# The end of the first slot in a four-stage kernel: batch 2's products, the weights and the transposed output in another order

## The chip, the cores and the metric

One core of a Trainium2 chip runs the whole program. The metric is the time of one execution on the device in microseconds, given as the median of several. The engines that matter here are TensorE (PE in the profile, with its weight loads as PEld), VectorE (DVE), ScalarE (ACT), GpSimd (POOL), and SyncE's queue (SP), from which most DMAs are issued. Each engine works through its own queue in order, and waits at an instruction until the semaphores that it needs are set.

## The reference

The input is four batches of 512 rows by 256 columns in fp32. Each is normalised and passed through four sublayers, each added to its own input:

```python
x = x + attn_a(layernorm(x))     # windows
x = x + ffn(layernorm(x))
x = x + attn_b(layernorm(x))     # causal attention
x = x + ffn(layernorm(x))
```

`attn_a` cuts a batch into tokens of 16 channels, makes q, k, v of each, and attends within windows of eight tokens in two branches (eight along one axis for the first eight channels, eight along the other for the rest). A 3x3 depthwise convolution of v is added, and the result is projected by a 16x16 matrix, normalised over its 16 channels and added to the normalised input. `ffn` has 2048 hidden units; gate, up and down weights are 4-bit codes with a scale for each block of 32:

```python
gate = einsum('th,nh->tn', xt, Wg);  up = einsum('th,nh->tn', xt, Wu)
out = einsum('tn,hn->th', gelu(gate) * up, Wd)
```

`attn_b` has 16 heads of 16 channels, with rotary positions and a causal mask.

## The kernel before, in words

All four batches stay in SBUF as `X[b]` ([128, 4, 256]). The weights are unpacked once, on VectorE, into `Wf`: twelve words (`WORDS`, L720: g0, u0, ... d2, d3), each of six VectorE steps and two DMA loads from SP's queue (`dequant`, L722). The buffers of the later words come from pools with two turns, so that a word's loads wait until the word two before it has been used up.

The work is laid out in slots. In a slot TensorE runs one batch's FFN pass (`ffn`, L824) while the other engines work on another batch's windows:

- before the slots: batch 0's windows, alone
- first slot: FFN of batch 0 (pass f0), windows of batch 1, the start of batch 2's windows, and the second half of the weights (`first_slot`, L1393)
- two further slots: FFN of batch 1 with the windows of batch 2 (pass f1), FFN of batch 2 with those of batch 3
- then the remaining FFN passes with the causal attention beside them

A pass has two halves of eight hidden tiles. For tile n, TensorE makes `pg_n` (gate) and `pu_n` (up), each of two 128x512 matmuls (two records each in the trace); ScalarE applies gelu to `pg_n` into `gs_n`; VectorE multiplies `it_n = pu_n * gs_n` (L866 in the first slot, L868 later). At the end of a half, four `po` groups of eight 128x256 matmuls take all eight `it`, and VectorE adds each `po` to X (L897). `pg`, `pu` and `po` share three PSUM banks in turn (pool `ps3`, L69): a tile may be written only when the tile three before it has been read. So gate tile n+2 waits for `it_n`.

The windows of a batch are: `window_front` (statistics of the 16-token rows, normalisation, transposes `yTp`, q, k, v and convolution into T); `window_parts` (L433), that is products of q and k (`tq`), folded into scores (`sc`), their maximum (`mx`), exponentials (`ek`), weighting of v (`tv`), and sums into `att`; `window_back` (L640), that is for each half a transpose `aTp` (L655), a copy `aT` by ScalarE (L657), a projection (L661), and statistics; then `turn` (a root by Newton steps on 128x64, scalings, and `z`), `move` (`zp`: 64 narrow matmuls that bring z into X's layout, L700) and `add` (X <- X + zp, L711). `norm_rows` (L759) makes the next pass's input of X: four statistics (L771, L772), the root (L777 and, on GpSimd, L778), four `xn` (L789), their transposes `xTp` (L809), and ScalarE's copies `xT` (L812, L813).

Sums over eight products are made in one of two ways: by VectorE, folding halves (`fold`, `values_here`), or on TensorE, piling eight products and the convolution up in a PSUM bank by matmuls with the identity (`pile`, `values_piled`, L588). In the first slot, the values of branch 1, half 0, are piled in the bank `va1`.

What sets the order: in the first slot the queues of TensorE and VectorE are written out by hand, with a planner. `Pace` (L104) keeps two running times, `pe` and `dve`. VectorE work is booked with `spend` (L126), which lets the pass take further steps (`steps`, each `each` us of TensorE) as long as `pe` is behind `dve`, and issues an `it` when its due time has come. `matmuls` books other TensorE work. `fill` (L1409) puts weight steps (`pieces`) among the products up to a cap on the number made, `want` makes a word at the latest when the pass needs it, and `step` advances the front of batch 2. After the first slot, `weave` (L1220) writes out TensorE's queue alone, and the other engines' queues follow a scheduler; `queue_behind` (L1232) ties an instruction behind another in the issue order, with no wait of its own. `beside_window` (L1491) runs `window_middle` (L609), whose first products of batch b are tied behind `state[b - 1, "moved"]` (the last z) for half 0 and behind `state["f..."]` (the last `xn` of the coming pass) for half 1.

Of the kernel before, what the change touches and what calls it, by code (L numbers as in the profile page):

```python
# [14 lines left out]
ALU = mybir.AluOpType  # L15
# [20 lines left out]
def hybrid_kernel(  # L36
# [25 lines left out]
    nc = tc.nc  # L62
# [80 lines left out]
    def paced(us):  # L143

        if pace:
            pace[0].spend(us)
            if pace[0].fill is not None:
                pace[0].fill()
# [138 lines left out]
    def window_front(a1, a2, c, b, y, state):  # L287
# [12 lines left out]
        if b in (1, 2):  # L300

            junk = a1.tile([P, P], F32, tag="junk", name=f"junka{b}")
            for s in range(8):
                if b == 2 and s == 4:
                    yield 2.5
                nc.scalar.activation(junk, y[:, s, :], AF.Identity, accum_out=mv[:, s, 0:1])
            yield 3.5
            ps = over_halves(0, mv[:, :, 0])
            nc.scalar.activation(mean, ps, AF.Copy, scale=-1.0 / P)
            yield 1.0  # L310
            for s in range(8):
                if b == 2 and s == 4:
                    yield 2.5
                nc.scalar.activation(
                    junk, y[:, s, :], AF.Square, bias=mean[:, s : s + 1], accum_out=mv[:, s, 1:2]
                )
            yield 3.5
            nc.scalar.activation(off, over_halves(1, mv[:, :, 1]), AF.Copy, scale=1.0 / P)
            inv_root(rs, off)
            nc.gpsimd.tensor_tensor(mean, mean, rs, ALU.mult)  # L320
            yield 3.0
        else:
            for s in range(8):
                st = a2.tile([P, 6], F32, tag="st", name=f"sta{b}_{s}")
                nc.vector.bn_stats(st, y[:, s, :])
                nc.vector.bn_aggr(mv[:, s, :], st)
            yield 3.5
            if b == 0:
                busy(8)
            mm = over_halves(0, mv.rearrange("p s t -> p (s t)")).rearrange("p (s t) -> p s t", t=2)  # L330
            nc.vector.tensor_tensor(off, mv[:, :, 0], mm[:, :, 0], ALU.subtract)
            nc.vector.tensor_tensor(off, off, off, ALU.mult)
            nc.vector.scalar_tensor_tensor(off, off, EPS, mm[:, :, 1], ALU.add, ALU.add)
            nc.gpsimd.tensor_tensor(rs, off, mhalf, ALU.pow)

            yield 4.0
            yield 4.0
            behind = last_on(mybir.EngineType.DVE).name
            ins = nc.vector.scalar_tensor_tensor(mean, mm[:, :, 0], -1.0, rs, ALU.mult, ALU.mult)
            if b > 1:  # L340
                queue_behind(ins, behind)
# [42 lines left out]
        for hf in range(2):  # L384
# [13 lines left out]
            for s in range(max(lo - 1, 0), min(hi + 1, 7) + 1):  # L398
                t0, t1 = max(0, lo - s + 1), min(3, hi + 2 - s)
                at = 384 + 16 * (s - 1 - lo)  # L400
# [32 lines left out]
    def window_parts(a1, a2, c, b, state):  # L433
# [22 lines left out]
        def pile(dst, parts):  # L456
            for n, part in enumerate(parts):
                nc.tensor.matmul(dst, ident, part, start=n == 0, stop=n == len(parts) - 1)  # L458
# [127 lines left out]
            paced(0.35)  # L586

        def values_piled(br, hf, at=None):  # L588
            part = tmp["v", br, hf]
            if at is not None:  # L590
                got["va", br] = at
            dst = bank("va", br)[:, 256 * hf : 256 * hf + 256]
            own = T[:, hf, 7 - br]
            pile(dst, [part(k, k + 1)[:, :, 0] for k in range(8)] + [own])

        def take_piled(br, hfs):
            rows = slice(4 * hfs[0], 4 * hfs[-1] + 4)
# [11 lines left out]
    def window_middle(a1, a2, c, b, state):  # L609

        w = window_parts(a1, a2, c, b, state)

        def late(br):

            behind = last_on(mybir.EngineType.Activation).name
            queue_behind(w["power"](br), behind)

        for br in range(2):
            for hf in range(2):
                ins = w["products"](br, hf)  # L620
                if br == 0:

                    queue_behind(ins, state[b - 1, "moved"] if hf == 0 else state[f"f{b - 1}"])
                w["scores_here"](br, hf)
                yield 4.6
            w["peak"](br)
            yield 1.4

        late(0)
        late(1)  # L630
        for br in range(2):
            w["total_here"](br)
            w["shares"](br)
            yield 2.3
            for hf in range(2):
                w["weighted"](br, hf)
                w["values_here"](br, hf)
                yield 5.1
# [593 lines left out]
    def queue_behind(ins, name):  # L1232

        tc.add_manual_dep(
            ins.ins, name,
            mybir.DependencyInfo(mybir.DependencyClass.NoSync, mybir.DependencyReason.DATA),
            reason="issue order",
        )
# [12 lines left out]
    def drain(work):  # L1251
        for _ in work:
            pass
# [37 lines left out]
    with ExitStack() as left:  # L1291
# [101 lines left out]
        def first_slot():  # L1393


            run = Pace()
            run.each = 0.9
            run.main = ffn(f1, i1, 0, got[0], "f0", False, False, later=run)
            xa = window_load(a2, 2)
            other = window_front(a1, a2, wconst, 2, xa, state)  # L1400
            w = window_parts(a1, a2, wconst, 1, state)
            first_made = made[0]

            def pieces(n, us=0.6):
                for _ in range(n):
                    if next(words, None) is not None:
                        run.spend(us)

            def fill():  # L1409

                while made[0] < min(0.8 * run.dve + first_made - 4.0, 66):
                    pieces(1)

            def want(name):
                while made[0] < 6 * WORDS.index(name) + 6:
                    next(words)
                    run.dve += 0.6

            run.want = want

            def step(costs=[0.0, 0.0, 0.2, 0.0, 0.0, 0.2, 0.0, 0.0, 0.9, 3.7, 2.5]):
                next(other, None)
                if costs:
                    run.matmuls(costs.pop(0))

            pace.append(run)
            run.fill = fill
            for br in range(2):
                for hf in range(2):
                    w["products"](br, hf)  # L1430
                    w["scores_here"](br, hf)
                    step()
                w["peak"](br)
                step()
            behind = last_on(mybir.EngineType.Activation).name
            queue_behind(w["power"](0), behind)
            queue_behind(w["power"](1), last_on(mybir.EngineType.Activation).name)
            pieces(4)
            for br in range(2):
                w["total_here"](br)  # L1440
                w["shares"](br)
                if br == 0:
                    step()
                for hf in range(2):
                    w["weighted"](br, hf)
                    if br == 0:
                        step()
                    if (br, hf) == (1, 0):
                        w["values_piled"](br, hf, one("va1"))
                        run.matmuls(4.2)  # L1450
                        w["take_piled"](br, (hf,))
                        continue
                    if (br, hf) == (1, 1):
                        project, turn, move, add = window_back(a1, a2, wconst, 1, state)
                        first, second = project(0), project(1)
                        next(first)
                        run.matmuls(0.5)
                    w["values_here"](br, hf)
                    if br == 0:
                        step()  # L1460
            next(first)
            run.matmuls(0.9)
            next(second)
            run.matmuls(0.5)
            run.fill = None
            next(first, None)
            next(second)
            run.matmuls(0.9)
            run.limit = 96
            pieces(72 - made[0])  # L1470
            next(second, None)
            next(second, None)
            drain(turn())
            run.spend(6.2)
            move()
            run.matmuls(3.8)
            pieces(72)
            run.limit = 96
            run.spend(max(0.0, run.pe - run.dve))
            add()  # L1480
            run.spend(1.2)
            for _ in norm_rows(f1, 1, "f1", got, aside=lambda: run.spend(2.0)):
                run.spend(0.45)
            run.room(0)
            pace.clear()
            for _ in run.main:
                pass
            run.room(0)
            del state["due"]
# [146 lines left out]
```

## Time and profile before

| | |
|---|---|
| median of 3 runs | 1032.29 us (1028.6 to 1038.07) |
| profiled execution | 1030.32 us, of which its span 1028.4 us |
| busy: PE, DVE, ACT, POOL | 98%, 65%, 34%, 13% of the span |
| granted TensorE clock, mean | 0.991 |
| first slot's pass on TensorE | from 82.3 us to 193.1 us |
| HBM traffic | 12.32 MB read, 2.10 MB written |

A row of a timeline gives start and length in us, engine, line, operation, output and inputs with their shapes, the number of records, and in brackets the idle time before it and what ended that. TensorE's rows overlap a little where matmuls are pipelined. A row of the waits gives who waited for whom, the total in us, the number of times and the longest. In a table by stretches the clock is the share of full speed that TensorE was granted.

### The profile page before, as it was taken

Reading aid. Unit: us, or ns where it says so; the run is one execution under the profiler, and the core shown is the slowest. Engines: PE = TensorE matmul, PEld = TensorE weight load, DVE = VectorE, ACT = ScalarE, POOL = GpSimd, SP = SyncE. Lnnn points to the kernel's source line nnn. Section 1 sums busy time; section 2 is a strip of 40 time slices with the busy share of each in tenths; the row PEclk is TensorE's granted clock in tenths of the full one; section 3 lists DMA queues with packets and bytes.
Section 4 is the critical chain, followed back from the end, with each engine's and each line's share of the span. In section 5 each row is a group of like instructions: output and inputs, shape, how many; then the busy total and the mean of one; then the engine's idle time right before and its main releaser. Section 6 shows DMA issues by size and latency. Waiting matters only on the chain.

```text
span 1028.4 us, 14319 instructions
## 1 busy us (share of the span) xinstructions
PE 1005.5 (98%) x5574; PEld 596.2 (58%) x5574; DVE 670.7 (65%) x1589; ACT 350.9 (34%) x603; POOL 132.4 (13%) x259
## 2 busy tenths in 40 slices
PE   7989999899999999999999999999999999999998
PEld 7864657565756475564474554664644746446556
DVE  6978999958866777847477555776465575543111
ACT  3543251142212213434524445235254253461110
POOL 3100000000000012011330112311113201120000
PEclk8999999999999999999999999999999999999999
DMA  7210110000000020000000000000000000000000
GB/s 184 68 43 21 41 42 7 15 1 1 2 1 1 0 68 1 1 1 1 2 1 0 2 1 1 6 16 1 1 1 1 21 0 1 1 1 21 1 0 21
DMA packets 14403, 15.33 MB, mean 15 GB/s; under 512 B 2352, under 2 KB 10840, under 8 KB 14304
## 3 DMA queue, kind: packets, MB, share of 16 engines
q1 hardware_dynamic: 12416, 13.31, 4.4%
q10 hardware_dynamic: 1568, 1.06, 0.4%
q8 instruction: 44, 0.72, 0.3%
q0 software_dynamic: 352, 0.06, 0.1%
q14 instruction: 23, 0.19, 0.1%
HBM read 12.32 MB, written 2.10 MB: 14 GB/s over the span
## 4 chain that ended last, share of the span: by engine, by line
PE 92%; DVE 5%; ACT 1%; POOL 0%; issue 0%; DMA 0%; SPq 0%; POOLq 0%; DVEq 0%; ACTq 0%
PE pg_s L836 11%; PE pu_s L857 11%; PE pg_f L836 11%; PE po_s L882 11%; PE pu_f L857 10%; PE po_f L882 10%; PE s L1046 5%; PE o L1131 4%; PE sT L1095 4%; PE qkv_b L985 3%; PE va L458 2%; PE qkT L1022 1%; PE qkv_b L989 1%; PE zp L700 1%; PE qkv L402 1%; PE qkv L390 1%
## 5 line engine op out<-in xcount | busy, mean ns | idle before, releaser
L1061 DVE CUSTOM_DVE_ANT_0 junk<-s,mask 128x512 f32<-128x512 f32 (+3 forms) x256 | 110.1, 487 | 36.9 <-PE s L1046 19.8
L836 PE MATMUL pg_s<-xT_s,g 128*128 128x512 f32 x256 | 126.7, 603 | 0.0
L857 PE MATMUL pu_s<-xT_s,u 128*128 128x512 f32 x256 | 125.4, 601 | 0.0
L836 PE MATMUL pg_f<-xT_f,g 128*128 128x512 f32 x256 | 123.9, 599 | 0.7 <-ACT xT_f L812 0.7
L857 PE MATMUL pu_f<-xT_f,u 128*128 128x512 f32 x256 | 122.8, 595 | 0.0
L882 PE MATMUL po_s<-d,it_s 128*128 128x256 f32 x512 | 118.0, 382 | 0.0
L882 PE MATMUL po_f<-d,it_f 128*128 128x256 f32 x512 | 117.8, 383 | 0.0
L882 PEld LDWEIGHTS po_s<-d,it_s 128*128 128x128 f32 x512 | 95.2, 190 | 20.8 <-issue 8.8
L882 PEld LDWEIGHTS po_f<-d,it_f 128*128 128x128 f32 x512 | 96.0, 191 | 18.1 <-issue 5.9
L1111 POOL TENSOR_SCALAR_AFFINE_SELECT e<-e 128x256 f32<-128x256 f32 x128 | 52.7, 424 | 344.7 <-ACT e L1107 341.8
L1107 ACT ACTIVATE e<-sT 128x1024 f32<-128x1024 f32 (+1 forms) x72 | 66.5, 969 | 72.0 <-PE sT L1095 72.0
L836 PEld LDWEIGHTS pg_s<-xT_s,g 128*128 128x128 f32 x256 | 45.9, 190 | 56.8 <-issue 50.9
L857 PEld LDWEIGHTS pu_f<-xT_f,u 128*128 128x128 f32 x256 | 47.1, 190 | 54.1 <-issue 51.8
L857 PEld LDWEIGHTS pu_s<-xT_s,u 128*128 128x128 f32 x256 | 46.1, 190 | 54.4 <-issue 50.2
L836 PEld LDWEIGHTS pg_f<-xT_f,g 128*128 128x128 f32 x256 | 46.6, 190 | 51.8 <-issue 47.4
L848 ACT ACTIVATE gs_f<-pg_f 128x512 f32<-128x512 f32 x48 | 28.6, 596 | 138.6 <-PE pg_f L836 130.0
L845 DVE SCALAR_TENSOR_TENSOR g_s<-g_s,gs_s 128x512 f32<-128x512 f32 x48 | 33.2, 691 | 59.1 <-ACT g_s L844 58.7
L842 ACT COPY gs_s<-pg_s 128x512 f32<-128x512 f32 x48 | 28.2, 587 | 67.7 <-PE pg_s L836 67.5
L1046 PE MATMUL s<-kT,qT 16*128 16x384 f32 (+3 forms) x512 | 50.0, 467 | 0.0
L897 DVE TENSOR_TENSOR X<-po_s,X 128x256 f32<-128x256 f32 (+1 forms) x33 | 13.5, 413 | 54.0 <-PE po_s L882 54.0
L1131 PE MATMUL o<-e,V 128*32 128x256 f32 (+3 forms) x512 | 44.4, 441 | 0.4 <-PE sT L1095 0.4
L868 DVE TENSOR_TENSOR it_f<-pu_f,gs_f 128x512 f32<-128x512 f32 x32 | 21.9, 687 | 31.7 <-PE pu_f L857 31.6
(233 smaller groups left out, 1365.3 us busy)
## 6 DMA issues: line engine op xcount, KB each, us to landing
X<-in_x_dram SPq DMA_DIRECT2D x4, 512.0 KB
out_dram<-X SPq DMA_DIRECT2D x15, 128.0 KB
xa<-in_x_dram SPq DMA_DIRECT2D x28, 64.0 KB
pkg<-in_gate_p_dram SPq DMA_DIRECT2D x4, 256.0 KB
sbg<-in_gate_s_dram SPq DMA_DIRECT2D x4, 256.0 KB
pku<-in_up_p_dram SPq DMA_DIRECT2D x4, 256.0 KB
sbu<-in_up_s_dram SPq DMA_DIRECT2D x4, 256.0 KB
pkd<-in_down_p_dram SPq DMA_DIRECT2D x4, 256.0 KB
```

Of the source, the lines that this page charges most:

```text
L836: nc.tensor.matmul(pg, Wf["g"][par][q][:, o : o + P], xT[:, par, :], start=par == 0, stop=par == 1)
L845: nc.vector.scalar_tensor_tensor(g2, g2, 1.0, gs, ALU.add, ALU.mult)
L848: nc.scalar.activation(gs, pg, AF.Gelu_apprx_tanh)
L857: nc.tensor.matmul(pu, Wf["u"][par][q][:, o : o + P], xT[:, par, :], start=par == 0, stop=par == 1)
L882: nc.tensor.matmul(po[:, 0:W], inter[k][:, i * P : (i + 1) * P], Wf["d"][par][j // 2][:, (j % 2) * W : (j % 2 + 1) * W], start=k == 0, sto ...
L985: nc.tensor.matmul(ps[:, 0, :], xT[:, par, rows], c["wqk"][:, :, par], start=par == 0, stop=par == 1)
L1046: nc.tensor.matmul(pss[hl // 2][:, hl % 2, at : at + n], qT[h0 : h0 + HD, g, i * P : (i + 1) * P], kT[h0 : h0 + HD, g, 0:n], start=True, s ...
L1061: nc.vector.tensor_tensor_reduce(out=junk[:, 0:n], in0=pss[k][:, hl % 2, at : at + n], in1=c["mask"][:, 512 - n : 512], scale=1.0, scalar= ...
L1095: nc.tensor.matmul(pss[hl // 2][:, hl % 2, at : at + n], kT[h0 : h0 + HD + 1, g, kt * P : (kt + 1) * P], qT[h0 : h0 + HD + 1, g, kt * P : ...
L1107: nc.scalar.activation(e[:, :, 0 : 512 - at0], pss[k][:, :, at0:512], AF.Exp)
L1111: nc.gpsimd.affine_select(out=diag, in_=diag, pattern=[[0, 2], [1, P]], compare_op=ALU.is_ge, fill=0.0, base=0, channel_multiplier=-1,)
L1131: nc.tensor.matmul(outs[g][h0 : h0 + 32, kt * P : 512], v[:, kt, 4 * g + hl, :], e[:, hl % 2, at : at + n], start=kt == 0, stop=kt == 2,)
```

## The change

It has six parts, all but the first two inside `first_slot`:

- In the statistics of batch 3's windows (`window_front`), each first instruction is tied behind `state["f1"]`, the last `xn` for batch 1's FFN pass.
- In `window_middle`, batch 2's half 0 products are tied behind that `xn` too, as half 1 already was; batch 3's stay tied behind z.
- In the values of branch 1, half 0, VectorE first adds the upper four products to the lower four, and TensorE piles four instead of eight.
- The planner's constants: a pass step counts 0.88 instead of 0.9, `pe` starts at 2.5 instead of 0, and the cap of `fill` is 72 instead of 66, so that all weights can be made among the products.
- After the products, the second projection is emitted whole before any weights that are left.
- `move` comes only after the pass has made 89 of its 96 steps.

```diff
-                nc.vector.bn_stats(st, y[:, s, :])
+                ins = nc.vector.bn_stats(st, y[:, s, :])
+                if b == 3:
+                    queue_behind(ins, state["f1"])
...
         def values_piled(br, hf, at=None):
-            part = tmp["v", br, hf]
+            part, keys = tmp["v", br, hf], 8
             if at is not None:
-                got["va", br] = at
+
+                got["va", br], keys = at, 4
+                nc.vector.tensor_tensor(part(0, 4), part(0, 4), part(4, 8), ALU.add)
+                paced(1.2)
...
-            pile(dst, [part(k, k + 1)[:, :, 0] for k in range(8)] + [own])
+            pile(dst, [part(k, k + 1)[:, :, 0] for k in range(keys)] + [own])
...
-                    queue_behind(ins, state[b - 1, "moved"] if hf == 0 else state[f"f{b - 1}"])
+                    queue_behind(ins, state[b - 1, "moved"] if hf == 0 and b > 2 else state[f"f{b - 1}"])
...
-            run.each = 0.9
+            run.each, run.pe = 0.88, 2.5
...
-                while made[0] < min(0.8 * run.dve + first_made - 4.0, 66):
+                while made[0] < min(0.8 * run.dve + first_made - 4.0, 72):
...
-                        run.matmuls(4.2)
+                        run.matmuls(2.4)
...
             run.matmuls(0.9)
-            run.limit = 96
+            drain(second)
             pieces(72 - made[0])
-            next(second, None)
-            next(second, None)
             drain(turn())
             run.spend(6.2)
+            while run.steps < 89:
+                run.spend(0.2)
             move()
             run.matmuls(3.8)
-            pieces(72)
-            run.limit = 96
             run.spend(max(0.0, run.pe - run.dve))
             add()
```

## The prediction

> **What bounds the kernel now.** First the page's busy shares: TensorE is busy nearly throughout.
>
> ```profile
> span 1028.4 us, 14319 instructions
> PE 1005.5 (98%) x5574; PEld 596.2 (58%) x5574; DVE 670.7 (65%) x1589; ACT 350.9 (34%) x603; POOL 132.4 (13%) x259
> ```
>
> So only 22.9 us of the span are without a matmul, and a reordering that adds no matmul can win from these or from slow matmuls. Next, who TensorE waited for between 82 us, where the first slot's pass starts, and 300 us:
>
> ```profile
> PE xTp_f L809 <- DVE xn_f L789: 4.4, 1, 4.4
> PE aTp L661 <- ACT aT L657: 1.4, 2, 0.7
> PE pg_f L836 <- ACT xT_f L812: 0.7, 1, 0.7
> PE aTp L655 <- ACT att L598: 0.5, 1, 0.5
> ```
>
> All but the 0.7 (at 82 us, ahead of the slot) lie in the first slot's end. That stretch of TensorE's timeline (start, length, operation, and in brackets the wait before it):
>
> ```profile
> 153.71 1.12 PE L857 MATMUL pu_f<-xT_f,u 128*128 128x512 f32 x2
> 154.91 3.69 PE L458 MATMUL va<-tv,ident 128*128 128x256 f32 x16
> 158.44 0.59 PE L458 MATMUL va<-T,ident 128*128 128x256 f32 x2
> 159.50 0.66 PE L655 MATMUL aTp<-ident,att 128*128 128x128 f32 x4 [0.46 <-ACT att L598]
> 160.83 1.16 PE L661 MATMUL aTp<-pw,aT 128*128 128x128 f32 x8 [0.68 <-ACT aT L657]
> ...
> 163.16 1.16 PE L661 MATMUL aTp<-pw,aT 128*128 128x128 f32 x8 [0.73 <-ACT aT L657]
> ...
> 176.31 3.70 PE L700 MATMUL zp<-z,sel 128*32 128x128 f32 x128
> 179.94 3.72 PE L882 MATMUL po_f<-d,it_f 128*128 128x256 f32 x16
> 188.09 0.66 PE L809 MATMUL xTp_f<-ident,xn_f 128*128 128x128 f32 x2 [4.43 <-DVE xn_f L789]
> 188.55 1.92 PE L882 MATMUL po_f<-d,it_f 128*128 128x256 f32 x4
> ```
>
> After `zp` there are eight `po` matmuls, then 4.43 us of nothing. Why is `xn` late? VectorE's timeline shows batch 2's product standing between the last projection and the sum X<-X,zp, and later batch 3's statistics alternating with the rows':
>
> ```profile
> 177.60 2.28 DVE L476 TENSOR_TENSOR tq<-T 128x2048 f32<-128x2048 f32 x1
> ...
> 181.99 1.21 DVE L711 TENSOR_TENSOR X<-X,zp 128x1024 f32<-128x1024 f32 x1
> ...
> 187.53 1.38 DVE L789 TENSOR_SCALAR xn_f<-X,mv_f,rs_f 128x256 f32<-128x256 f32 x4 [0.80 <-POOL rs_f L778]
> ```
>
> `zp` ended at 180.0; the sum could have begun then and began at 181.99. The busy time by stretch (stretch, its length, TensorE busy and its instructions, granted clock, DMA share, GB/s) shows the wait's second price in its clock column:
>
> ```profile
> 184.00:188.00 4.00, 0.00 (x0) 0.97 0.05 14
> 188.00:190.00 2.00, 1.91 (x6) 0.50 0.00 0
> 190.00:192.00 2.00, 2.00 (x10) 0.71 0.00 0
> ```
>
> **What the Trainium skill says.** "TensorE: Matmul & The Clock Gate", Part 1 (The HAM clock gate): half clock after about 3.4 us of idleness, full clock after about 3.4 us of work, in a free-running window. The trace agrees: 0.50 after the 4.43 us wait, full by 192. The same page, Part 4 (PE-mode transpose), says transposes do not count as busy in the same way; no row here tests that alone. But the trace shows a drop to 0.50 at 76 to 78 us without an empty gap of that length, behind a 0.95 us wait and many narrow matmuls. "DVE: scalar operands, raw-bit mode, write accounting and state across instructions", section 5 (Flops that outlive an instruction), says VectorE's queue is in order; the trace agrees, the sum at 181.99 standing behind the 2.28 us product.
>
> **The change, part by part.** "Before" and "after" orders are those of the two programs' queues; durations are start to start from the rows above.
>
> *Half of one pile on VectorE.* Of `va`'s nine matmuls for (1, 0) four go: 16 records take 3.53 us, so 8 x 0.44, and four are 1.77 us off TensorE. VectorE gains one addition of 128x1024, 1.13 us (128x1024 rows at L580 stand at 1.22, next one 1.13 later). The pile now stands behind `pu_15`. Laying VectorE's new queue end to end, that addition ends at about 158.2, TensorE reaches the pile at about 159: covered, by 0.8; uncovered it would cost at most 1.1. ("(1, 0)" is the second branch's first half.)
>
> *Weights and FFN steps between the projections.* The products of d3 (four integer steps and two scalings, 3.2 us on VectorE) move from between the projections (164.3) into the value products. They are paid by the slot's start: before, VectorE waited 3.40 us ahead of the first `it` at 86.32; after, a 2.2 us product stands there. d3's two loads are released by u3's last scaling, near 136.5 instead of 138.4; before, the DMA was moving bytes until about 142.5, 4 us after issue, so they land near 140.6, and are needed near 142.6. SP's other loads keep their order. Four and two `po` matmuls (0.43 each: 1.7 and 0.9 us) now stand between each transpose and its projection. The copy of `aT` takes 0.59 and about 0.1 of signalling, so the 0.68 + 0.73 = 1.41 us go; the 0.46 for `att` stays, nothing standing behind `va`.
>
> *z later.* `zp` follows 24 `po` matmuls instead of 18, and eight stay behind it, with all eight transposes after them. With the projections at about 165 and 167.5, the last statistic ends near 169.6, and the root, scalings and both z take 6.2 us (170.90 to 177.1 before): z_0 near 174.1, z_1 near 175.8, `zp` due near 175.2 and its second half near 177. Hidden, with about 1 us over.
>
> *Products and statistics behind the rows.* The path from `zp` to the transposes is then: to the sum 0.07, sum to statistics 1.26, four statistics with their aggregates 2.26 (in the first stage, where nothing stood between: 72.05, 73.31, 75.57), one X addition before them 0.34, the root on GpSimd 1.27 (186.26 to 187.53), `xn` to the first transpose 0.56 (187.53 to 188.09): 5.76. TensorE has 3.45 us of `po` for it: a wait of about 2.35 in place of 4.43. The four `xn` come 0.33 apart, so the transposes take 1.25 instead of 1.04 (+0.21), and the copy of `xT`, hidden by `po` before, is bare: 0.68, as at 82.34.
>
> *What is queued behind.* At the next pass's start VectorE now owes batch 2's tq_0_0 (4.3 with its folds), most of tq_0_1 (3.3) and eight statistics (2.0) that were done before. The pool `ps3` has three banks, so gate tile n+2 cannot start before `it_n` has read pu_n, and TensorE gets there 3.44 us after pu_n's end. From the first `xn` on: the `xn` and an X addition 1.65, tq_0_0 with folds and two statistics 4.4, `it_0` 0.65, sc 0.35, the other statistics 1.75, tq_0_1 and folds 3.95, `it_1` 0.6, together 13.35. TensorE is at gate tile 3 after 0.56 + 1.25 + 0.68 + 3 x 3.44 = 12.8: 0.55 too early, taken as 0.6. Later `it` come in time, since VectorE had 2.67, 2.74 and 3.62 us of waits before 222, so the debt is paid before the exponentials at 222.5. Cost 0.6, between 0 and 1.2.
>
> *The clock.* From the end of `po` to the next pass it is 2.35 + 1.25 + 0.68 = 4.3 us with only transposes in it. A drop costs half of 3.4 us of matmuls plus some slow transposes, 2.0 at most; none costs 0. Both ends have a precedent, so I take 1.0.
>
> *The sum.* Gone: 1.77 + 1.41 + 4.43, and the half clock: 188.09 to 193.09 is 5.00 for six `po` (2.59) and eight transposes (1.04), so 1.37; together 8.98. Come: 2.35 + 0.21 + 0.68 + 0.6 + 1.0 = 4.84. Net 4.1 off. Everything later is bound by TensorE and moves up with it. The profiled execution took 1030.32 (span and 1.9 around it), so 1026.2. It lay 2.0 below the median of the runs shown, 1032.29; the same step from there is 1028.2. I take the middle, 1027.
>
> **The rivals.**
> 1. *The clock stays up and no `it` is late*: 1.6 more, and switching losses near the removed waits (some 0.6 of the stretch is neither matmul nor listed wait) go too: about 6.5 off; from the profile 1024, and down to 1021 if the chain after `zp` is shorter. For: a 2.35 us gap is under what dropped the clock. Against: the drop at 76 us.
> 2. *The wait only changes its name*: z is late by the 1.5 that the projections slip, or d3's loads hold VectorE; each takes 1 to 2 us, the clock drops: 0 to 2 off, 1029 to 1031. For: VectorE pauses once, for 0.6, between 87 and 160. Against: the margins above.
> 3. *Slower: `it` late all through the first slot.* The planner now starts TensorE's count 2.5 us later and steps it by 0.88, so each `it` stands about one VectorE instruction later (it_0 behind the 2.2 us product). TensorE stops once an `it` misses its 3.44 us. Over 16 gate tiles a miss of 0.6 each is 9.6, against 4.1: 1030.3 + 5.5 = 1036. It wins from a mean miss of 0.26. Against: laid end to end, the queue leaves 1 to 2 us for nearly all, 0.25 for `it_9`.
>
> **How the numbers follow.** Forecast 1027, chance 0.68; rival 1 0.13; rival 2 0.12; rival 3 0.07. The range of 1021 to 1032 takes in rival 1, rival 2 and the 2 us between profile and median. About 1% is what a measurement of this kernel can tell from no change: under 1022.0 lies part of rival 1 and the luck of a median, 0.12; over 1042.6 only a rival 3 worse than priced, 0.03; the rest 0.85.
>
> **What would show it.** Right: `va` with 10 records for (1, 0); no wait ahead of the projections' matmuls; the wait for `xn` near 2.3 and a bare one near 0.7 for `xT`; one wait of about 0.6 by a bank in the next pass. Wrong: several short waits in the pass between 85 and 145, a wait ahead of `zp`, or a wait for `xn` still above 4.

## The result and the profile after

| | before | after |
|---|---|---|
| median, runs of both taken side by side | 1032.73 us (1026.79 to 1041.73) | 1027.37 us (1021.68 to 1032.97) |
| ratio | | 0.9943, 95% interval 0.9922 to 0.9965 |
| profiled execution's span | 1028.4 us | 1030.5 us |
| first slot's pass, from its first gate matmul to the next pass's | 110.75 us | 104.47 us |

The change takes 0.57% off, 5.9 us of 1032.7 with an interval of 3.6 to 8.1. (The ratio is estimated from all the runs; the two medians themselves lie 5.4 apart.) The profiled execution of the changed kernel, however, has a longer span than that of before, with TensorE busy for 1.3 us less:

```profile
span 1030.5 us, 14308 instructions
PE 1004.2 (97%) x5566; PEld 594.9 (58%) x5566; DVE 672.8 (65%) x1590; ACT 350.9 (34%) x603; POOL 134.0 (13%) x259
```

A profile is one execution, and so its span has to be cut up before it is compared. Three pieces do: from the span's start to the first gate matmul of the pass f0; from there to the first gate matmul of the pass f1 ("the stretch" from here on); the rest. In the two profiles they are 82.34 + 110.75 + 835.31 and 90.69 + 104.47 + 835.34. The first piece, in which the change alters no engine's queue, scatters: two further executions of the changed kernel entered the pass at 81.19 and 86.52, with a stretch of 104.47 and 104.46 and a rest of 835.34 and 835.32 (spans of 1021.0 and 1026.3). The stretch repeats within 0.02 in the changed kernel; of the kernel before there is one profile. Between these executions the change is worth 6.28 us, and the timed interval of 3.6 to 8.1 holds that.

Who TensorE waited for in the changed kernel between 90 and 300 us:

```profile
PE xTp_f L814 <- DVE xn_f L794: 2.0, 1, 2.0
PE pg_f L841 <- ACT xT_f L817: 1.4, 2, 0.7
PE aTp L660 <- ACT att L603: 0.5, 1, 0.5
PE va L460 <- DVE tv L595: 0.2, 1, 0.2
```

The wait for `xn` has fallen from 4.4 to 2.0, the two for `aT` are gone, that for `att` stays. New are a second 0.7 for `xT` (the first stands ahead of the slot in both kernels) and 0.2 ahead of the pile. TensorE's timeline of the slot's end has the same in its brackets:

```profile
167.66 1.97 PE L460 MATMUL va<-tv,ident 128*128 128x256 f32 x8 [0.18 <-DVE tv L595]
...
170.52 0.66 PE L660 MATMUL aTp<-ident,att 128*128 128x128 f32 x4 [0.46 <-ACT att L603]
171.01 1.89 PE L887 MATMUL po_f<-d,it_f 128*128 128x256 f32 x8
172.74 1.05 PE L666 MATMUL aTp<-pw,aT 128*128 128x128 f32 x8
...
183.82 3.70 PE L705 MATMUL zp<-z,sel 128*32 128x128 f32 x128
187.46 3.72 PE L887 MATMUL po_f<-d,it_f 128*128 128x256 f32 x16
193.17 1.32 PE L814 MATMUL xTp_f<-ident,xn_f 128*128 128x128 f32 x8 [1.99 <-DVE xn_f L794]
195.16 1.12 PE L841 MATMUL pg_f<-xT_f,g 128*128 128x512 f32 x2 [0.68 <-ACT xT_f L817]
```

VectorE's timeline there shows the new order: no work for another batch stands between z and the sum, so that VectorE now waits for `zp` (the 2.53). Then comes only the rows' own work and an addition of `po`, and the product of batch 2 stands behind the last `xn`:

```profile
187.59 1.22 DVE L716 TENSOR_TENSOR X<-X,zp 128x1024 f32<-128x1024 f32 x1 [2.53 <-PE zp L705]
...
192.61 1.38 DVE L794 TENSOR_SCALAR xn_f<-X,mv_f,rs_f 128x256 f32<-128x256 f32 x4 [1.12 <-POOL rs_f L783]
...
194.24 2.28 DVE L478 TENSOR_TENSOR tq<-T 128x2048 f32<-128x2048 f32 x1
```

And the stretches of 2 us (TensorE busy, instructions, clock, DMA share, GB/s) show a clock of 1.00 in the gap and behind it, where before had 0.50 and 0.71 behind its own:

```profile
192.00:194.00 2.00, 0.83 (x6) 1.00 0.00 0
194.00:196.00 2.00, 1.32 (x6) 1.00 0.00 0
196.00:198.00 2.00, 2.00 (x6) 1.00 0.00 0
```

The 6.28 in two parts, all counted from the pass's first gate matmul. `zp` begins at 93.13 where it began at 93.97, though six more `po` (6 x 0.43 = 2.59) stand ahead of it: 3.43 are gone from what comes before. From `zp` to the next pass it is 11.34 instead of 16.78, 5.44 less; 2.59 of that are the six `po` that moved ahead, so 2.85 are gone there. 3.43 + 2.85 = 6.28.

### The profile page after: what moved, and what is told of

It is laid out like the page before. It is cut to its first block, busy times and chain, and to the rows that moved or that the text cites. A ratio compares the mean times of both kernels' runs of the same rounds, so it can differ in the third digit from the quotient of the medians.

```text
span 1030.5 us, 14308 instructions
## 1 busy us (share of the span) xinstructions
PE 1004.2 (97%) x5566; PEld 594.9 (58%) x5566; DVE 672.8 (65%) x1590; ACT 350.9 (34%) x603; POOL 134.0 (13%) x259
## 4 chain that ended last, share of the span: by engine, by line
PE 90%; DVE 5%; DMA 1%; POOL 1%; issue 1%; ACT 1%; POOLq 0%; DVEq 0%; ACTq 0%
PE pg_s L841 11%; PE pu_s L862 11%; PE po_s L887 11%; PE po_f L887 11%; PE pg_f L841 10%; PE pu_f L862 9%; PE s L1051 5%; PE o L1136 4%; PE sT L1100 4%; PE qkv_b L990 3%; PE zp L705 1%; PE va L460 1%; PE qkT L1027 1%; PE qkv_b L994 1%; DMA pbrow<-in_proj_b_dram 1%; PE idle L433 1%
## 5 line engine op out<-in xcount | busy, mean ns | idle before, releaser
L1051 PEld LDWEIGHTS s<-kT,qT 16*128 16x128 f32 x512 | 23.1, 183 | 32.5 <-issue 11.6
```

The costliest lines, as they stand in the source:

```text
L1051: nc.tensor.matmul(pss[hl // 2][:, hl % 2, at : at + n], qT[h0 : h0 + HD, g, i * P : (i + 1) * P], kT[h0 : h0 + HD, g, 0:n], start=True, s ...
```

## The experiments

The theory is that the gain has three sources, each with its place: the pile and the filled projections (ahead of `zp`), the ties on VectorE (between `zp` and the next pass), and the clock (behind the gap). The rivals gave all of it to one part, or said that what leaves one wait comes back in another. The experiments take the parts one by one. This table holds what their profiles gave; "by the profile" is the sum of stretch and rest less that of before, 110.75 + 835.31. Rows without a ratio were profiled and not timed.

| kernel | stretch | rest | by the profile | ratio to before, 95% interval |
|---|---|---|---|---|
| after | 104.47 | 835.34 | -6.25 | 0.9943 (0.9922 to 0.9965) |
| the ties alone | 106.62 | 835.31 | -4.13 | 0.9952 (0.9929 to 0.9976) |
| after without the ties | 107.87 | 837.52 | -0.67 | 0.9987 (0.9962 to 1.0011) |
| after, `zp` behind all `po` | 109.43 | 837.12 | +0.49 | 1.0011 (0.9988 to 1.0033) |
| after, `zp` behind 22 `po` | 103.43 | 835.30 | -7.33 | 0.9934 (0.9911 to 0.9957) |
| after, `zp` behind 20 `po` | 103.41 | 835.35 | -7.30 | |
| after with the whole pile, two executions | 105.77, 105.77 | 837.02, 838.39 | -3.27, -1.90 | |
| after with the cap of 66, two executions | 105.85, 105.85 | 837.00, 837.05 | -3.21, -3.16 | |
| after with the old planner constants | 105.26 | 835.35 | -5.45 | |

Each timed ratio lies within 0.1% of its row's -6.25, -4.13, -0.67, +0.49 and -7.33 divided by 1032, though one profile alone could not have shown it by its span. The intervals of the first two rows overlap, so the division of the gain among the parts rests on the traces and not on the timed runs.

**The ties alone.** To the kernel before, only what moves VectorE's instructions behind the last `xn`:

```diff
-                nc.vector.bn_stats(st, y[:, s, :])
+                ins = nc.vector.bn_stats(st, y[:, s, :])
+                if b == 3:
+                    queue_behind(ins, state["f1"])
...
-                    queue_behind(ins, state[b - 1, "moved"] if hf == 0 else state[f"f{b - 1}"])
+                    queue_behind(ins, state[b - 1, "moved"] if hf == 0 and b > 2 else state[f"f{b - 1}"])
```

> The kernel before with only the two ties (batch 2's products and batch 3's statistics behind the last xn); TensorE's order is the same as before. 'Stretch' is the time from the first pass's first gate matmul to the next pass's: 110.75 us before, 104.47 after. Theory (VectorE's order is what made xn late): the sum begins at zp's end, the chain to the first transpose is 5.42, eight po cover 3.45, so the wait for xn falls from 4.43 to about 1.8, the clock stays at 1.00 and the 1.37 of half clock go: stretch 106.8, the whole 4.0 faster. Rival (the clock drops all the same, a short wait being enough): stretch 108.1. Rival (the debt of 9 us on VectorE only moves the wait into the next pass): waits of TensorE above 2 us between the next pass's first gate matmul and 100 us later, the whole not faster.

TensorE's timeline of that kernel at the gap:

```profile
176.78 3.72 PE L884 MATMUL po_f<-d,it_f 128*128 128x256 f32 x16
182.29 0.41 PE L811 MATMUL xTp_f<-ident,xn_f 128*128 128x128 f32 x2 [1.79 <-DVE xn_f L791]
```

The wait is 1.79 instead of 4.43 (2.64 less), the pair of transposes behind it takes 0.41 instead of 0.66, and the half clock with its 1.37 is gone: 4.01 of the 4.13 that the stretch lost (the shorter transposes are part of the 1.37). Not one wait appears in the 100 us behind it, though VectorE owes the same products and statistics as in the changed kernel. The ties alone thus carry two thirds of the gain, and what they put off costs nothing: the rest took 835.31, as before.

**The other four parts without the ties.** To the kernel after, the same two places as they were before:

```diff
-                ins = nc.vector.bn_stats(st, y[:, s, :])
-                if b == 3:
-                    queue_behind(ins, state["f1"])
+                nc.vector.bn_stats(st, y[:, s, :])
...
-                    queue_behind(ins, state[b - 1, "moved"] if hf == 0 and b > 2 else state[f"f{b - 1}"])
+                    queue_behind(ins, state[b - 1, "moved"] if hf == 0 else state[f"f{b - 1}"])
```

> The changed kernel without the two ties; only VectorE's order differs from after: tq_0_0, its folds and two statistics stand before the sum again, and statistics alternate with the rows'. Theory: of 4.7 us of such work 2.5 fit into VectorE's wait ahead of the sum, so the sum comes 2.1 later, the rows' statistics 2 later again: the wait for xn rises from 1.99 to about 6.0, the clock drops to half, worth about 1.5 more: stretch about 110, as long as before, so the ties carry nearly all of the gain in this order, the whole within 2 us of the kernel before. Rival (the pile, the weights and the place of zp carry the gain, the ties little): stretch below 107.

Two rows of TensorE's timeline of that kernel:

```profile
186.67 1.83 PE L812 MATMUL xTp_f<-ident,xn_f 128*128 128x128 f32 x8 [4.91 <-DVE xn_f L792]
189.18 3.78 PE L839 MATMUL pg_f<-xT_f,g 128*128 128x512 f32 x4 [0.68 <-ACT xT_f L815]
```

The wait grew to 4.91, less than the 6.0 expected. The sum came 2.3 later, about as expected, but from the sum to the root it took 4.3 instead of 3.7, only 0.6 more where 2 had been expected. Behind this wait the clock fell (0.50 from 187 to 193), and unlike in the kernel before no `po` stood between the transposes to be slowed in place of the gate matmuls: the eight transposes take 1.83 instead of 1.32, four gate records 3.78 instead of 1.98. The stretch keeps 2.88 of the gain, and 2.2 of that go again in the rest. So the pile and the filled projections are worth what they save only together with the ties; of their 3.4 us ahead of `zp`, 0.7 arrives.

**The pile.** To the kernel after, all eight products piled, no addition:

```diff
-                got["va", br], keys = at, 4
-                nc.vector.tensor_tensor(part(0, 4), part(0, 4), part(4, 8), ALU.add)
+                got["va", br] = at
```

> The changed kernel with eight products piled on TensorE instead of four plus an addition; all else stands as in after. Theory: four 128x256 matmuls of 0.44 more, less the 0.18 wait for the addition: stretch 104.47 + 1.6 = 106.1, z and zp both 1.6 later. Rival (TensorE had slack at the pile, VectorE's addition being what it waits for): stretch within 0.3 of 104.5.

The stretch grew by 1.30, both times that this kernel was profiled. The row `va<-tv` has 16 records and 3.62 us instead of 8 and 1.97 (1.65 more). Against this the pile begins 0.35 earlier, at 76.62 from the pass's start (156.23 less 79.61) and not at 76.97; the wait of 0.18 ahead of it, now gone, is part of that. The addition therefore was not quite covered; it cost 0.35 of its 1.1.

**The weights.** To the kernel after, the cap of `fill` as before, and the rest of the weights ahead of the second projection's remainder:

```diff
-                while made[0] < min(0.8 * run.dve + first_made - 4.0, 72):
+                while made[0] < min(0.8 * run.dve + first_made - 4.0, 66):
...
+            pieces(72 - made[0])
             drain(second)
-            pieces(72 - made[0])
```

> The changed kernel with the old cap of 66 on weight steps and so the six steps of d3 (3.2 us) made after the second projection instead of among the products. Theory: the statistics and z come about 3.2 later, z had about 1.0 to spare ahead of zp, and TensorE waits about 2 us for z or for d3: stretch 106.5 to 107. Rival (the weights' place is free, VectorE having enough waits at the end): stretch within 0.5 of 104.5.

(By the edit the six steps stand between the second projection's first part and its remainder. The 66 and 72 count steps of weights; the later expectations' "66 products" are these.)

The size was near (105.85), but not for the reason given: nothing waited for z or for d3. The planner put FFN steps elsewhere, and the second projection waited for `aT` again, as before:

```profile
160.04 1.16 PE L666 MATMUL aTp<-pw,aT 128*128 128x128 f32 x8 [0.73 <-ACT aT L662]
```

With 0.24 for `yT` and 0.34 instead of 0.18 ahead of the pile, waits make 1.13 of the 1.38. What the cap of 72 buys is FFN steps at the places where the projections need them.

**The planner's constants.** To the kernel after:

```diff
-            run.each, run.pe = 0.88, 2.5
+            run.each = 0.9
```

> The kernel after with the planner's two constants of the kernel before: 0.9 per small step instead of 0.88, and no 2.5 of start for TensorE's count; nothing is left out. It moves only instructions of TensorE: the last of yTp one FFN step later, two po ahead of va, the second half of po around k. Theory (the two constants only keep the planner's count in step with the other edits): all waits as in the kernel after within 0.3 each, the stretch 104.3 to 105.3. Rival (the constants carry a part of the gain, by keeping FFN steps in stock for the end): a new wait of over 0.7 at va, att or aT, the stretch over 105.5.

The stretch was 105.26, at the end of what the theory allowed, and with a wait of 0.76 ahead of the pile that the rival had named; 0.16 came ahead of `zp`. Two `po` stood ahead of the pile where the changed kernel has FFN tiles, and TensorE reached the pile before the addition was done. The constants carry 0.8 of the 6.28.

The sixth part, the loop that holds z until 89 steps are made, moves nothing: a program built without it has the same queues on all engines. `zp` stands behind 18 `po` before and with the ties alone, and behind 24 in the changed kernel and in the four variants of it that leave this place alone. Which of the other edits moves it, no run separates.

**Where `zp` stands.** Three kernels hold the pass at other numbers of steps. For `zp` behind all 32 `po`:

```diff
+            run.limit = 96
             run.spend(6.2)
-            while run.steps < 89:
+            while run.steps < 96:
                 run.spend(0.2)
...
+            run.limit = 96
             for _ in norm_rows(f1, 1, "f1", got, aside=lambda: run.spend(2.0)):
```

> The kernel after with zp behind all 32 po, nothing of them between zp and the transposes; nothing is left out. Theory: the eight po were all the cover of the chain from zp to xTp (5.76), so the wait of xTp grows from 1.99 by their 3.45 to 5.4, and the stretch from 104.47 to 107.9; behind a gap this long the clock goes to a half as in the kernel before, which costs 1.3 to 1.7 more by pm of batch 3 (115.73 becomes 120.5 to 121). Ratio 0.998 to 1.000. Rival (TensorE is ahead of VectorE here, the chain begins with VectorE's work on the values and not with zp): the wait grows by far less than 3.45 and the stretch stays under 106.

Its timeline of TensorE:

```profile
171.78 3.72 PE L887 MATMUL po_f<-d,it_f 128*128 128x256 f32 x16 [0.83 <-DVE X L902]
...
184.57 1.94 PE L814 MATMUL xTp_f<-ident,xn_f 128*128 128x128 f32 x8 [5.44 <-DVE xn_f L794]
187.18 3.75 PE L841 MATMUL pg_f<-xT_f,g 128*128 128x512 f32 x4 [0.68 <-ACT xT_f L817]
```

The wait is 5.44 in TensorE's timeline, as the theory had it, and the half clock is back. The stretch is 1.5 above the 107.9 expected, by a wait that was not thought of (0.83: the fourth `po` group needs a bank that VectorE reads out late, busy with z) and by 0.6 for transposes at half clock. The order "z late" loses the whole gain of the change when its cover is gone.

For `zp` behind 22, the same lines with limits of 91 and 95, so that the last two `po` stand behind the transposes:

> The kernel after with one shift in the end of the first slot: zp stands behind 22 of the 32 po instead of 24, and the last two po stand behind the transposes. Nothing is left out. Between zp and the transposes lie eight po, as in the kernel after. Theory (the wait of xTp is set by the chain that starts at zp, 5.76 us less the po that stand behind zp): xTp's wait stays at 1.99 within 0.2, and the two po (0.86) lie over the copy of xT, so that the bare 0.68 ahead of pg goes: the stretch from pass to pass falls from 104.47 to 103.8, and with work between the transposes and pg the clock stays at 1.00. Rival (VectorE is late: it has the sum of the output's last rows ahead of the statistics, and the earlier zp finds it busy): the wait grows by the 0.86 that zp is earlier, to 2.85, and the stretch is 104.6. Ratio to the kernel before: 0.9935 against 0.994.

Its timeline of TensorE:

```profile
185.68 1.32 PE L814 MATMUL xTp_f<-ident,xn_f 128*128 128x128 f32 x8 [1.78 <-DVE xn_f L794]
186.83 1.03 PE L887 MATMUL po_f<-d,it_f 128*128 128x256 f32 x4
```

The two `po` behind the transposes take the place of the bare 0.68 for `xT`, which is gone as expected (no bracket stands ahead of the next gate matmul); the wait fell to 1.78 because one addition to X now stands behind the rows' statistics instead of ahead of them. Together the stretch is 1.04 shorter than in the changed kernel. The timed ratios of the two (0.9934 and 0.9943) are too near each other to tell them apart; the stretch does.

And with limits of 90 and 95 (by the queue `zp` stood behind 20 and ten `po` followed, one more than the expectation says):

> zp behind 21 of the 32 po, nine po between it and the transposes, the last two behind them; nothing is left out. Theory (the chain from zp to the transposes, some 5.3 us with the eight po's 3.45 and a wait of 1.78 in the kernel with 22, sets the wait): one po more between them takes 0.43 from the wait, to 1.35, and from the stretch, to 103.0. Rival (VectorE's z of the second half, which ends 1.15 before it is needed in the kernel after, is late for a zp that comes three po, 1.29, earlier): a wait of some 0.2 inside zp and a stretch of 103.2; TensorE then gains no more from an earlier zp.

Its timeline of TensorE:

```profile
181.31 3.70 PE L705 MATMUL zp<-z,sel 128*32 128x128 f32 x128 [0.81 <-DVE z L687]
...
190.43 1.31 PE L814 MATMUL xTp_f<-ident,xn_f 128*128 128x128 f32 x8 [0.91 <-DVE xn_f L794]
```

The rival was right in kind, with a wait of 0.81 for its 0.2: 0.81 ahead of `zp` and 0.91 ahead of `xTp` make 1.72, where the kernel with 22 had 1.78 in one piece, and the stretches are 103.41 and 103.43. With `zp` any earlier than behind 22, the end is set by VectorE's root and z.

**The clock.** Behind the gap of 1.99 + 1.32 of transposes + 0.68 the clock stayed at 1.00 in the changed kernel and fell in the two variants with the whole pile and with the cap of 66, whose gap and whose queue from `zp` on are the same. Each was profiled again.

> The changed kernel once more, for its profile. Theory (the clock looks at fixed windows that don't start with the kernel, so the same gap of 1.99 + 1.3 of narrow transposes + 0.68 is seen in one execution and not in another): the stretch is 104.47 within 0.1 again, and pm of batch 3 comes either at 115.7 (clock 1.00) or at 117.4 (clock at a half for some 3.5 us after the gap, as in the two kernels with the same gap). Rival (the drop belongs to those two kernels' own order): 115.7 and a clock of 1.00 again; this one run can speak for the rival only weakly, but a drop settles it against the rival.

> The kernel with the pile of eight parts once more, for its clock. The first time its clock went to a half behind the gap of 1.99 + 1.3 + 0.68 and pm of batch 3 came 118.73 after the first gate matmul, 12.96 after the next pass's. Theory (the clock looks at windows whose phase is another in each execution): the stretch is 105.77 within 0.1 again; the clock can stay at 1.00 this time, with pm 11.2 to 11.3 after the pass's start, or fall again. Rival (the order of this kernel makes it fall): 12.9 again. 11.3 settles it against the rival, 12.9 leaves it open.

> The kernel with 66 window products ahead of the slot's end once more, for its clock. The first time the clock fell and pm of batch 3 came 12.96 after the next pass's first gate matmul. Theory (phase of the execution): stretch 105.85 within 0.1; pm 11.2 to 11.3 or 12.9 after the pass's start. Rival (the order): 12.9 again.

> The changed kernel a third time, for its clock. So far, with the same gap of 1.99 + 1.3 + 0.68 behind the same eight po and the same zp, the clock stayed at 1.00 in the changed kernel (twice) and with the old constants of the planner (once), and fell with the whole pile (twice, for different lengths: pm of batch 3 came 12.96 and 14.29 after the next pass's start) and with 66 products (twice, 12.96). Theory (the phase of the execution against the clock's windows): the stretch is 104.47 within 0.1, pm 11.26 or 12.9 to 14.3 after the pass's start, each about as likely. Rival (something in those two kernels ahead of the gap makes it fall): 11.26 again. A fall settles it against the rival; 11.26 leaves it open.

It fell twice in two with the whole pile and twice in two with 66, and stayed up three times in three in the changed kernel and once with the old constants. Its cost was not the same in one and the same kernel: from the pass's first gate matmul to `pm` of batch 3 it took 12.96 the first time and 14.29 the second, against 11.26 at full clock, so 1.7 or 3.0 us.

The traces say more than these totals. In each of the fourteen, the times at which the granted clock changes lie whole multiples of 3.413 us apart, on a grid that stands elsewhere against the program in each execution. That fits a window of activity that runs free of the program; the Trainium skill's page "TensorE: Matmul & The Clock Gate", Part 1 (The HAM clock gate), says so and names about 3.4 us. Cut at this grid, the second execution with the whole pile and then the profiled one of the changed kernel read (length, TensorE busy, instructions, clock, DMA share, GB/s):

```profile
185.49:188.90 3.41, 1.42 (x9) 1.00 0.00 1
188.90:192.31 3.41, 2.73 (x4) 0.50 0.00 0
192.31:195.73 3.42, 3.42 (x5) 0.50 0.00 0
195.73:199.14 3.41, 3.41 (x9) 1.00 0.00 0
```

```profile
188.99:192.40 3.41, 2.19 (x11) 1.00 0.29 77
192.40:195.82 3.42, 1.98 (x10) 1.00 0.00 0
195.82:199.23 3.41, 3.41 (x10) 1.00 0.00 0
```

The transposes are 1.28 of the 1.42 and 1.32 of the 1.98. So the window ahead of the fall held 0.14 us of other matmuls, and the emptiest one where the clock stayed up held 0.66. At this place all fourteen executions divide in the same way: in the seven that fell (before, without the ties, `zp` behind all 32, whole pile twice, 66 twice) the window ahead of the fall held at most 0.54, and in the seven that stayed up no window over the gap held less than 0.66. The page's section speaks of an idle window; here one with 0.54 us in it was enough. With the transposes counted there is no such division: one execution with 66 fell with 1.86, and the one with the old constants stayed up with 1.66.

So where the grid meets the gap decides, which speaks for the theory's phase and against the order of the two kernels. No run set the phase; that all four falls came in those two kernels is by this account chance. The cost follows too: the half clock lasted one window, 3.41 us, in the three executions that lost 1.7, and two in the one that lost 3.0. The account is for this place only: ahead of the pass, among narrower matmuls, the clock fell behind windows from 57 to 79 us that held 1.9 to 2.5 us of them.

Two things follow for the totals. The changed kernel has the same gap of 3.98 us and can fall too; an estimate from 3.41, 3.98 and a limit between 0.54 and 0.66 is that about half of all phases make it fall. And before's one profile lost one window, where those without the ties and with `zp` behind all 32 lost two, so that totals of kernels that fall are good to some 1.3 us only.

## Why the prediction was right

The forecast of 1027 us met 1027.37, and the sign and most steps were right; but the sum promised 4.1 us and the change gave 6.28. That it came within 0.4 us is luck: a sum that was 2.1 short was taken from a point 1 us below the median. The forecast came close because it was set at the middle between the profile less 4.1 and the median less 4.1, and so 5.3 below the median shown. Since the stretch repeats within 0.02 us and the scatter lies ahead of it, the right way was to take the stretch's difference from the median: 1032.29 less 6.28 is 1026.0, and from the median of the later runs, 1032.73, it is 1026.5.

- *The pile.* Right in what goes (four matmuls; the whole pile gave 1.30 back). "Covered, by 0.8" was not: it cost 0.18 of wait, some 0.35 in all. TensorE came to the pile 76.8 us after the pass's start, near the 76.7 said, but the addition ended at 76.8 instead of 75.9.
- *The filled projections.* Right: both waits for `aT` are gone and that for `att` stayed at 0.46. Ahead of `zp`, 3.43 were gained where 1.77 + 1.41 = 3.18 had been listed and 0.18 of new wait came. The 0.43 between may be the switching losses that only rival 1 counted; no run measured them alone. (The six steps of d3 take 3.45 on VectorE's timeline of before, not 3.2; nothing hung on it.)
- *d3 and z.* Right: neither made TensorE wait. `zp` was said to have about 1 us over; two `po` earlier (0.86) it still had no wait, four earlier 0.81.
- *The chain from `zp`.* Right: 5.76 was said, and it is 5.71, from 187.46 to 193.17: 0.13 to the sum, 1.47 to the statistics, 2.26 for these, 1.29 for the root and 0.56 to the transposes. The wait was 1.99 for 2.35, as the eight `po` end 3.72 after `zp`, not 3.45. The transposes and the bare `xT` were right (1.32 for 1.25; 0.68).
- *`it_1` late, 0.6.* Wrong, and not by its arithmetic. From the first `xn` (192.61) VectorE's queue to the end of `it_1` was to take 13.35 and took 13.54, and TensorE was to be at gate tile 3 after 12.8 and was there after 12.95. So `it_1` was indeed 0.59 late for that tile, but TensorE did not wait. The timelines of VectorE, ScalarE and TensorE:

```profile
205.49 0.66 DVE L873 TENSOR_TENSOR it_f<-pu_f,gs_f 128x512 f32<-128x512 f32 x1
```

```profile
204.05 0.60 ACT L853 ACTIVATE gs_f<-pg_f 128x512 f32<-128x512 f32 x1 [2.84 <-PE pg_f L841]
```

```profile
205.56 1.02 PE L841 MATMUL pg_f<-xT_f,g 128*128 128x512 f32 x2
...
207.50 1.88 PE L862 MATMUL pu_f<-xT_f,u 128*128 128x512 f32 x4
```

  Gate tile 3 begins at 205.56, while `it_1` still runs until 206.15. The step that failed is "The pool `ps3` has three banks, so gate tile n+2 cannot start before `it_n` has read pu_n". The same rule stands in the words on the kernel before. The banks are not handed out in a fixed turn. With `pu_1` still being read and `pu_2` just written, gate tile 3 can only stand in the bank of `pg_2`, which ScalarE's gelu had read by 204.65; in the program built it waits for that gelu alone, and `pu_3`, at 207.50, is the one behind `it_1`. It had 1.35 to spare there, and the rest of the program took 835.3 in every profile with a full clock.
- *The clock, 1.0.* A cost between 0 and 2 was right to carry and came out 0 in three executions, which by the grid above is their phase. Its upper end was too low: 3.0 in another kernel with the same gap.
- *The sum.* It was short by some 2.1: 1.0 for a clock that stayed up, 0.6 for `it_1`, 0.36 by the shorter wait, and about 0.2 that no run takes apart. Rival 1 (the clock stays up, no `it` late, "about 6.5 off") described what these executions did; it had been given 0.13. The step that was wrong as a mechanism is the bank rule. The clock's term was a stake between two outcomes, and the other one came.
- *Rivals 2 and 3.* Neither: z and d3 were in time, and in the first slot's pass no `it` held TensorE (between its start and the pile no wait is listed).

## What to carry to other kernels

When a wait stands at the end of an in-order queue, first ask which instructions of the waiting chain's engine do not belong to the chain: moving those alone gave two thirds of this gain, and the engine paid the debt within its slack. A step that is put off needs cover behind it as well as in front: with z behind all `po` the whole gain was lost, with two `po` kept for behind the transposes it grew. Cut a profile's span at two fixed instructions before comparing executions; here the stretch repeated within 0.02 us while the spans of one kernel differed by 9.5.

## What was not expected of the hardware

- Nearly all the scatter between three executions of the changed kernel lay in their first 81 to 91 us; from the pass's first matmul to the end they took 939.81, 939.81 and 939.78. What scatters ahead of the pass was not looked into.
- In each of the fourteen traces the granted clock changed only at points whole multiples of 3.413 us apart. At the slot's end it fell in just the seven executions in which one such window held at most 0.54 us of matmuls other than transposes; the others held 0.66 or more. A gap of 1.99 of wait, 1.32 of transposes and 0.68 of wait so took the clock to a half in four executions out of eight, and cost 1.7 to 3.0 us. In the three kernels that keep `po` among or behind the transposes, with a wait of at most 1.79, it did not fall.
